# Deformable sampling with its first product in PSUM and one turning matmul per sample, and expert choice with piecewise exponentials and four early weight groups

## The chip, the cores and the metric

The kernel runs on one core of a Trainium2 chip. A core has a matrix engine (TensorE, PE in the profile), VectorE (DVE), ScalarE (ACT), GpSimd (POOL) and SyncE (SP), which work side by side from queues of their own, each in order. SBUF is the working memory, PSUM the small memory into which TensorE writes, in eight banks of 2 KB per partition. The metric is device time in microseconds for one execution, the median of several runs.

## The reference

The program is a network of four layers on an image tensor x of shape (4, 128, 64, 64), in float32. Each layer adds a spatial part and a per-token part to x. The change touches the spatial part of layer 1 (a modulated deformable convolution) and the per-token part of layers 1 and 2 (expert choice). Cut to these:

```python
# layer 1, spatial: 9 taps k, per pixel an offset (dy, dx) and a mask
y0 = jnp.floor(py).astype(jnp.int32); x0 = jnp.floor(px).astype(jnp.int32)
ly = py - y0; lx = px - x0
v00 = sample(y0, x0);     v01 = sample(y0, x0 + 1)
v10 = sample(y0 + 1, x0); v11 = sample(y0 + 1, x0 + 1)
sampled = v00*(1-wy)*(1-wx) + v01*(1-wy)*wx + v10*wy*(1-wx) + v11*wy*wx
sampled = sampled * mask[:, None]
out = jnp.einsum('bckhw,ock->bohw', sampled, weight.reshape(O, C, KK)) + bias

# layers 1 and 2, per token: 64 experts choose 8 tokens each out of 4096
logits = jnp.einsum('bsd,ed->bse', x, gate_w) + gate_b
probs = jax.nn.softmax(logits, axis=1)
vals, idx = jax.lax.top_k(probs.transpose(0, 2, 1), K)
pooled = jnp.einsum('bked,bke->bed', gathered, topv)
h = jax.nn.gelu(jnp.einsum('ebd,edh->ebh', pooled_and_one, weight1), approximate=False)
out = jnp.einsum('ebh,eho->ebo', h_and_one, weight2)
# each expert's output, times topv, is added back at its 8 tokens
```

## The kernel before

The image stays in SBUF as `xs`, channels on the 128 partitions, in chunks of 512 pixels (8 chunks per image). The stages follow one another: involution, a recurrence, the deformable sampling, expert choice, a convolution, expert choice again, attention, and a last mixture of experts. The stages at hand keep the order of the source on TensorE, ScalarE, VectorE and GpSimd (`tc.manual_schedule(engines=ORDERED)`): what is written first is queued first on its engine, and semaphores order the engines among themselves.

**Deformable sampling** (`deformable`). For each image, `plan(b)` makes the normalised image, the offsets, the row indices `idx` and four weights `wq[0..3]` per pixel and tap, and writes a table to device memory in which one row of 512 floats holds the four neighbours of a pixel, 128 channels each. Then, for 8 chunks, 9 taps and 4 blocks of 128 pixels, `taken` gathers 128 rows by an indirect DMA into a tile `dcn_g` (one pixel per partition, L872; 1152 such gathers in all) and weights them. It works on a pair of blocks at a time:

- ScalarE multiplies neighbour 0 by its weight into an SBUF tile `dcn_one` (L886);
- VectorE multiplies neighbour 1 into a slot of the PSUM tile `dcn_part` (L889), adds neighbour 2 there (L892), and adds neighbour 3 with the result going to an SBUF tile `dcn_sum` (L897).

`joined` then lets TensorE turn both tiles, from pixels on partitions to channels on partitions, by products with the identity that add up in the PSUM tile `dcn_pt` (L912 and L913). Each float32 product appears in the profile as two matmul records. `turn_back` copies a full `dcn_pt` (four blocks) to `dcn_st` on ScalarE (L929), `convolve` multiplies by the tap's weights into `dcn_out` (L933), and `finish` adds the nine taps' sum to the image on VectorE (L939). The calls are delayed by a number of steps (`at(2, joined, ...)`, 6 for `turn_back`, 2 more for `convolve`, 4 more for `finish`), and after each step one small piece of `plan` for the next image is issued (`side`), so that squares, copies, transposes and the offset convolution of the next image lie between. `GATHERED` is the number of gather buffers. The PSUM banks are all taken: three for `dcn_pt`, two for `dcn_out`, two for `plan`, one for `dcn_part`.

**Expert choice** (`expert_choice`). Two images share one set of 128 partitions (64 experts each), called a pair p. Phase one makes layer-norm scales, the logits `chosen[p]` (128 x 4096), a table of tokens in device memory (`rows`), the eight largest per expert (`largest`), the softmax denominators (`exponentials`, L1164 for pair 0 in one instruction, L1170 for pair 1 in eight pieces), the gathered tokens (`ask`) and their weighted sums (`pool`). Phase two streams the experts' weights, 16 groups of four experts, two tiles of 1 MB per group (`load`, L1042 and L1044): `first`, `turn`, `second` and `hand` follow one another with a lag of one group each. `EARLY` groups are loaded in phase one into buffers of their own, and `LATE` more buffers exist in phase two only. Between the groups of phase two, `mark(p)` marks the eight largest logits and `choose(p)` turns them into exponentials, everything else into zero. For pair 0 the exponentials `exps` are those of phase one; for pair 1 they are made at g = 5 (L1334).

Of the kernel before, what the change touches and what calls it, by code (L numbers as in the profile page):

```python
# [17 lines left out]
F32 = mybir.dt.float32  # L18
# [3 lines left out]
AF = mybir.ActivationFunctionType  # L22
ALU = mybir.AluOpType
AX = mybir.AxisListType
# [4 lines left out]
P = 128  # L29
B, H, W = 4, 64, 64  # L30
N = H * W
CH = 512
NCH = N // CH
# [618 lines left out]
def deformable(net, sampling):  # L652
# [7 lines left out]
    tc, nc = net.tc, net.nc  # L660
# [2 lines left out]
    NO = 3 * KK  # L663
    Q4 = 4
    BANKS = {"pt": 3, "out": 2, "pd": 1, "pv": 1}
    GATHERED = 14
    tables, woff, boff = sampling.tables, sampling.woff, sampling.boff
    wk, bias, grids = sampling.wk, sampling.bias, sampling.grids
    with ExitStack() as ctx:
# [195 lines left out]
        def taken(m, two):  # L865


            rows, idx, wq, j, k = m
            gs = []
            for i in two:  # L870
                g = sb.tile([P, 4 * P], F32, name="dcn_g", tag="g", bufs=GATHERED)
                nc.gpsimd.indirect_dma_start(  # L872
                    out=g,
                    out_offset=None,
                    in_=rows,
                    in_offset=bass.IndirectOffsetOnAxis(ap=idx[:, j + i, k : k + 1], axis=0),
                )
                gs.append(g)

            def weight(q, i):  # L880
                return wq[q][:, j + i, k : k + 1]

            ones, sums = [], []
            for i, g in zip(two, gs):
                s = sb.tile([P, P], F32, name="dcn_one", tag="one", bufs=12)
                nc.scalar.activation(s, g[:, 0:P], AF.Copy, scale=weight(0, i))  # L886
                ones.append(s)
            for i, g in zip(two, gs):
                nc.vector.tensor_scalar_mul(parts[:, i % 2, :], g[:, P : 2 * P], weight(1, i))  # L889
            for i, g in zip(two, gs):  # L890
                part = parts[:, i % 2, :]
                nc.vector.scalar_tensor_tensor(  # L892
                    out=part, in0=g[:, 2 * P : 3 * P], scalar=weight(2, i), in1=part, op0=ALU.mult, op1=ALU.add
                )
            for i, g in zip(two, gs):
                s = sb.tile([P, P], F32, name="dcn_sum", tag="sum", bufs=11)
                nc.vector.scalar_tensor_tensor(  # L897
                    out=s,
                    in0=g[:, 3 * P : 4 * P],
                    scalar=weight(3, i),  # L900
                    in1=parts[:, i % 2, :],
                    op0=ALU.mult,
                    op1=ALU.add,
                )
                sums.append(s)
            return ones, sums

        def joined(pt, two, ones, sums):

            for i, one_, s in zip(two, ones, sums):  # L910
                out = pt[:, i * P : (i + 1) * P]
                nc.tensor.matmul(out, one_, net.ident, start=i == 0, stop=False)  # L912
                nc.tensor.matmul(out, s, net.ident, start=False, stop=i == 3)  # L913

        parts = ps.tile([P, 2, P], F32, name="dcn_part", bufs=1)
        with tc.manual_schedule(engines=ORDERED):
            for _ in plan(0):
                pass
            side = iter(())

            later = {}
            n = 0

            def at(lag, do, *args):
                later.setdefault(n + lag, []).append(partial(do, *args))

            def turn_back(k, pt, po, b, c):
                st = sb.tile([P, CH], F32, name="dcn_st", tag="st")
                nc.scalar.copy(st, pt)  # L929
                at(2, convolve, k, st, po, b, c)  # L930

            def convolve(k, st, po, b, c):
                nc.tensor.matmul(po, wk[:, k, :], st, start=k == 0, stop=k == KK - 1)  # L933
                if k == KK - 1:
                    at(4, finish, b, c, po)

            def finish(b, c, po):
                xo = net.chunk(b, c)
                nc.vector.scalar_tensor_tensor(out=xo, in0=po, scalar=bias, in1=xo, op0=ALU.add, op1=ALU.add)  # L939

            def step():
                nonlocal n
                n += 1
                for do in later.pop(n, ()):
                    do()
                next(side, None)

            for b in range(B):
                for _ in side:
                    pass  # L950
                side = plan(b + 1) if b + 1 < B else iter(())
                rows, idx, wq = made.pop(b)
                for c in range(NCH):
                    po = ps.tile([P, CH], F32, name="dcn_out", tag="out", bufs=BANKS["out"])
                    for k in range(KK):
                        pt = ps.tile([P, CH], F32, name="dcn_pt", tag="pt", bufs=BANKS["pt"])
                        for i in range(0, 4, 2):
                            two = (i, i + 1)
                            at(2, joined, pt, two, *taken((rows, idx, wq, 4 * c, k), two))
                            if i:  # L960
                                at(6, turn_back, k, pt, po, b, c)
                            step()
            while later:
                step()


def expert_choice(net, layer):
# [13 lines left out]
    tc, nc, ins = net.tc, net.nc, net.ins  # L981
# [4 lines left out]
    CG = P // EG  # L986
    PAIRS = B // 2
    K, ROW = 8, P + 16
    EARLY, LATE = 3, 2
    GONE = -3.0e38  # L990
    w1, w2 = ins[f"L{layer}_ffn_weight1"], ins[f"L{layer}_ffn_weight2"]
    with ExitStack() as ctx:
# [22 lines left out]
        chosen = [keep.tile([P, N], F32, name=f"moe_chosen{i}") for i in range(PAIRS)]  # L1015
        totals = [keep.tile([P, 1], F32, name=f"moe_total{i}") for i in range(PAIRS)]
        cgate = keep.tile([D, E], F32, name="moe_cgate")
        exps = keep.tile([P, N], F32, name="moe_exp")

        behind = keep.tile([P, 1], F32, name="moe_behind")  # L1020
        nc.gpsimd.memset(behind[0:E], 0.0)
# [5 lines left out]
        def mark(p):  # L1027
            lg = chosen[p]
            nc.vector.match_replace(out=lg, in_to_replace=tops[p], in_values=lg, imm_value=GONE)

        def choose(p):

            lg = chosen[p]
            nc.vector.scalar_tensor_tensor(
                out=lg, in0=lg, scalar=GONE, in1=exps, op0=ALU.is_equal, op1=ALU.mult
            )
# [11 lines left out]
        with (  # L1048
# [109 lines left out]
                nc.vector.tensor_copy(places[p], row)  # L1158
                nc.vector.tensor_scalar_mul(negs[p], top[:, 0:1], -1.0)

            def exponentials(p):

                if p == 0:
                    nc.scalar.activation(exps, chosen[p], AF.Exp, bias=negs[p], accum_out=totals[p])  # L1164
                else:
                    sums = sb.tile([P, NCH], F32, name="moe_sums", bufs=1)
                    for c in range(NCH):
                        sq = sb.tile([P, CH], F32, name="moe_sq", tag="moe_sq", bufs=5)
                        lg = chosen[p][:, c * CH : (c + 1) * CH]
                        nc.scalar.activation(sq, lg, AF.Exp, bias=negs[p], accum_out=sums[:, c : c + 1])  # L1170
                    nc.vector.tensor_reduce(totals[p], sums, AX.X, ALU.add)
                shares[p] = sb.tile([P, K], F32, name="moe_share", tag="moe_share")
                nc.scalar.activation(shares[p], tops[p], AF.Exp, bias=negs[p])

            def ask(p, j):
                if j == 0:
# [47 lines left out]
                if j % 3 == 0:  # L1224
                    rows(0, j // 3 - 2)
            scales(1)
            exponentials(0)
            inverted(1)
            for c in range(4, NCH):
                rows(0, c)  # L1230
            turn_scales(1)
            for c in range(NCH):
                logits(1, c)
                for n in (2 * c, 2 * c + 1):
                    rows(1 + n // NCH, n % NCH)
            largest(1)
            for c in range(NCH):
                rows(3, c)
                ask(0, c)
            exponentials(1)  # L1240
            for j in range(K):
                ask(1, j)
            pool(0)
# [9 lines left out]
        with (  # L1253
# [55 lines left out]
            def hand(g, out):  # L1309
                for p in range(PAIRS):  # L1310
# [5 lines left out]
                        stop=g == GROUPS - 1 and p == PAIRS - 1,  # L1316
                    )

            hs, t2, act, outs = {}, {}, {}, {}
            for g in range(GROUPS + 3):  # L1320
                if g < GROUPS:
                    hs[g], t2[g] = first(g)
                if 0 <= g - 1 < GROUPS:
                    act[g - 1] = turn(g - 1, hs.pop(g - 1))
                if 0 <= g - 2 < GROUPS:
                    outs[g - 2] = second(g - 2, act.pop(g - 2), t2.pop(g - 2))
                if 0 <= g - 3:
                    hand(g - 3, outs.pop(g - 3))
                if g == 2:
                    mark(0)  # L1330
                if g == 4:
                    choose(0)
                if g == 5:
                    nc.scalar.activation(exps, chosen[1], AF.Exp, bias=negs[1])  # L1334
                if g == 7:
                    mark(1)
                if g == 9:
                    choose(1)
            for p in range(PAIRS):
                nc.vector.tensor_add(ots[p], handed[:, p, :], b2)  # L1340
                nc.vector.tensor_scalar_mul(ots[p], ots[p], totals[p])
# [701 lines left out]
```

## Time and profile before

| what | value |
|---|---|
| median of 3 runs | 8143.69 us (8137.75 to 8143.82) |
| the profiled execution, its own time | 8494.04 us |
| its span, first to last instruction | 8492.0 us |
| granted TensorE clock, mean over the span | 0.936 |
| busy: PE, DVE, ACT, POOL | 90%, 65%, 44%, 62% |
| gathers of the sampling stage (L872), first to last start | 1311.3 to 3096.8 us |
| in 1311 to 3097 us: PE, DVE, ACT, POOL busy | 1204, 1246, 548, 1089 us |
| the same stretch: granted clock, DMA share, GB/s | 0.79, 0.63, 184 |
| expert choice of layer 1, phase one (3116 to 3239 us) | PE 104, DVE 45, ACT 72 us busy, DMA share 0.46 |
| expert choice of layer 1, phase two (3239 to 3318 us) | PE 61, DVE 27, ACT 21 us busy, DMA share 0.95 |

A line of the groups reads: line in the kernel, engine, operation, output and inputs, shape, count; then busy time in us and the mean of one in ns; then the idle time of the engine just before these instructions and what ended it. A line of the timeline reads: start in us, length in us, engine, line, operation, count of merged instructions, and in brackets the engine's idle time before it with what released it. The engine that is busiest over the whole span need not bound a stage: in the sampling stage no engine is busy more than 70% of the time, and the spacing of successive instructions has to be looked at. The profiled execution is one execution, and it is slower than the timed ones by 350.35 us.

### The profile page before, as it was taken

Reading aid. Unit: us, or ns where it says so; the run is one execution under the profiler, and the core shown is the slowest. Engines: PE = TensorE matmul, PEld = TensorE weight load, DVE = VectorE, ACT = ScalarE, POOL = GpSimd, SP = SyncE. Lnnn points to the kernel's source line nnn. Section 1 sums busy time; section 2 is a strip of 40 time slices with the busy share of each in tenths; the row PEclk is TensorE's granted clock in tenths of the full one; section 3 lists DMA queues with packets and bytes.
Section 4 is the critical chain, followed back from the end, with each engine's and each line's share of the span. In section 5 each row is a group of like instructions: output and inputs, shape, how many; then the busy total and the mean of one; then the engine's idle time right before and its main releaser. Section 6 shows DMA issues by size and latency. Waiting matters only on the chain.

```text
span 8492.0 us, 144746 instructions
## 1 busy us (share of the span) xinstructions
PE 7639.5 (90%) x58958; PEld 3304.7 (39%) x58958; DVE 5545.6 (65%) x8706; ACT 3707.0 (44%) x7214; POOL 5264.3 (62%) x3014
## 2 busy tenths in 40 slices
PE   8999985767676678988999999999999999999989
PEld 2222243444444444433344344443444434444333
DVE  7888755777777654235667667776776766777255
ACT  4444432333332332041555555555555555555511
POOL 5889704656566630000788788887888868888800
PEclk9999997888787788997999999999999999999999
DMA  5443206656566545032454454554454544555400
GB/s 176 93 86 78 62 8 177 199 165 209 166 202 185 173 146 202 0 114 77 87 111 103 102 108 101 108 109 99 106 110 106 104 103 101 107 110 109 101 24 24
DMA packets 298170, 966.23 MB, mean 114 GB/s; under 512 B 42508, under 2 KB 112652, under 8 KB 239644
## 3 DMA queue, kind: packets, MB, share of 16 engines
q0 software_dynamic: 143872, 673.55, 33.7%
q1 hardware_dynamic: 153628, 283.40, 11.8%
q8 instruction: 463, 7.59, 0.4%
q14 instruction: 207, 1.70, 0.1%
HBM read 469.14 MB, written 85.01 MB: 65 GB/s over the span
## 4 chain that ended last, share of the span: by engine, by line
PE 51%; DVE 2%; issue 1%; DMA 1%; ACT 0%; POOL 0%; SPq 0%; POOLq 0%; ACTq 0%; DVEq 0%; another core or an unknown queue 0%
PE att_pv L1647 15%; PE att_sc L1734 13%; PE att_mx L1591 10%; PE att_sc L1635 5%; PE top_po L1947 3%; PE top_pw L1923 1%; DVE att_most L1602 1%; DMA moe_w<-in_L_ffn_weight 1%; PE att_sc L1564 1%; PE att_sc L1695 0%; PE top_po L1945 0%; PE att_sc L1678 0%; PE att_mx L1489 0%; PE att_sc L1525 0%; PE att_sc L1591 0%
## 5 line engine op out<-in xcount | busy, mean ns | idle before, releaser
L1666 POOL TENSOR_TENSOR att_acc<-att_acc,att_ex 128x2048 f32<-128x2048 f32 x640 | 2904.3, 4538 | 638.9 <-ACT att_ex L1735 619.6
L1602 DVE TENSOR_REDUCE att_most<-att_mx 128x2 f32<-128x1024 f32 x2016 | 2462.4, 1222 | 1073.5 <-PE att_mx L1591 990.6
L1735 ACT ACTIVATE att_ex<-att_sc 128x512 f32<-128x512 f32 x4096 | 2222.9, 595 | 1777.0 <-PE att_sc L1734 1493.8
L1734 PE MATMUL att_sc<-att_q,att_k 32*128 32x512 f32 x8192 | 2456.7, 606 | 0.0
L1591 PE MATMUL att_mx<-att_k,att_q 32*128 32x512 f32 x8064 | 2293.4, 647 | 13.0 <-DVE att_parts L1614 10.9
L872 POOL DMA_INDIRECT dcn_g<-dcn_table,dcn_idx x1152 | 1090.1, 946 | 763.1 <-issue 235.4
L1635 PE MATMUL att_sc<-att_rows,att_ones_b 32*128 32x256 bf16 (+1 forms) x6144 | 1502.9, 306 | 4.7 <-ACT att_ex L1735 4.7
L1647 PE MATMUL att_pv<-att_ex,att_vals 128*32 128x256 f32 x16384 | 1310.3, 391 | 0.0
L1591 PEld LDWEIGHTS att_mx<-att_k,att_q 32*128 32x128 f32 x8064 | 611.6, 185 | 869.3 <-issue 709.9
L410 POOL TENSOR_TENSOR inv_prod<-inv_seen,inv_prod 128x512 f32<-128x512 f32 (+1 forms) x672 | 837.6, 1274 | 95.8 <-ACT inv_prod L409 95.8
L412 DVE SCALAR_TENSOR_TENSOR inv_prod<-inv_pk,bspan,inv_seen 128x512 f32<-128x512 f32 (+1 forms) x1120 | 774.6, 743 | 142.0 <-PE inv_pk L399 141.7
L1647 PEld LDWEIGHTS att_pv<-att_ex,att_vals 128*32 128x32 f32 x16384 | 322.6, 108 | 1319.7 <-issue 1301.6
L1734 PEld LDWEIGHTS att_sc<-att_q,att_k 32*128 32x128 f32 x8192 | 818.7, 183 | 11.0 <-issue 8.3
L912 PE MATMUL dcn_pt<-ident,dcn_one 128*128 128x128 f32 x2304 | 531.0, 314 | 241.1 <-issue 108.6
L913 PE MATMUL dcn_pt<-ident,dcn_sum 128*128 128x128 f32 x2304 | 529.9, 312 | 157.5 <-issue 108.4
L409 ACT ACTIVATE inv_prod<-inv_pk,bspan 128x512 f32<-128x512 f32 (+1 forms) x672 | 436.1, 682 | 505.7 <-PE inv_pk L399 495.8
L912 PEld LDWEIGHTS dcn_pt<-ident,dcn_one 128*128 128x128 f32 x2304 | 440.0, 223 | 511.1 <-issue 313.5
L929 ACT COPY dcn_st<-dcn_pt 128x512 f32<-128x512 f32 x288 | 166.2, 577 | 880.4 <-remote 457.2
L399 PE MATMUL inv_pk<-inv_red,wtap 32*96 32x512 f32 (+1 forms) x3584 | 512.7, 638 | 7.4 <-DVE wtap L377 7.4
L897 DVE SCALAR_TENSOR_TENSOR dcn_sum<-dcn_g,dcn_w,dcn_part 128x128 f32<-128x128 f32 x1152 | 354.0, 345 | 253.1 <-remote 138.4
L421 PE MATMUL inv_out<-inv_prod,inv_fold 96*32 96x512 f32 (+1 forms) x3584 | 478.5, 605 | 8.5 <-DVE xs L429 8.5
L913 PEld LDWEIGHTS dcn_pt<-ident,dcn_sum 128*128 128x128 f32 x2304 | 413.8, 222 | 179.8 <-issue 116.5
(355 smaller groups left out, 7260.2 us busy)
## 6 DMA issues: line engine op xcount, KB each, us to landing
att_sum<-att_ex POOLq DMA_DIRECT2D x320, 1024.0 KB
inv_seen<-inv_image SPq DMA_DIRECT2D x256, 266.0 KB
moe_w<-in_L_ffn_weight SPq DMA_DIRECT2D x64, 1024.0 KB
dcn_table<-dcn_xt SPq DMA_DIRECT2D x32, 1024.0 KB
att_sum<-att_ex SPq DMA_DIRECT2D x32, 1024.0 KB
att_sum<-att_acc POOLq DMA_DIRECT2D x32, 1024.0 KB
dcn_g<-dcn_table,dcn_idx POOLq DMA_INDIRECT x1152
moe_table<-moe_xt SPq DMA_DIRECT2D x64, 288.0 KB
```

What stands on the lines that cost most here:

```text
L410: nc.gpsimd.tensor_mul(of, view, of)
L412: nc.vector.scalar_tensor_tensor(out=of, in0=as_shape(pk[0:m], of), scalar=by, in1=view, op0=ALU.add, op1=ALU.mult)
L872: nc.gpsimd.indirect_dma_start(out=g, out_offset=None, in_=rows, in_offset=bass.IndirectOffsetOnAxis(ap=idx[:, j + i, k : k + 1], axis=0),)
L912: nc.tensor.matmul(out, one_, net.ident, start=i == 0, stop=False)
L913: nc.tensor.matmul(out, s, net.ident, start=False, stop=i == 3)
L1591: nc.tensor.matmul(pm[i] if alone else pm[:, i, :], q[r, t * P : (t + 1) * P], ks[r, kc * CH : (kc + 1) * CH], start=True, stop=True,)
L1602: nc.vector.tensor_reduce(most[:, 2 * half : 2 * half + 2, kc], pm, AX.X, ALU.max)
L1635: nc.tensor.matmul(pe[:, cols], ones_b[r], lows[g][r, cols], start=cols.start == 0, stop=False)
L1647: nc.tensor.matmul(block["pv"][r, cols], vals[b][:, t, r], ex[:, h, cols], start=t == 0 and half == 0, stop=t == NT - 1 and half == 1,)
L1666: nc.gpsimd.tensor_add(block["acc"], block["acc"], ex)
L1734: nc.tensor.matmul(pe, ks[r, t * P : (t + 1) * P], qs[c][r], start=False, stop=True)
L1735: nc.scalar.activation(ex[:, h, :], pe, AF.Exp)
```

## The change

In the sampling, ScalarE's product of neighbour 0 goes into a slot of `dcn_part`, which has four slots instead of two. VectorE adds neighbours 1 and 2 there, and neighbour 3 with the result to `dcn_sum`. `dcn_one` is gone, and TensorE turns one tile per sample. The ring of `dcn_sum` grows from 11 to 15 tiles and that of the gathers from 14 to 16.

In the expert choice, pair 0's exponentials are made in eight pieces, four between the `rows` of pair 0 and four between the `logits` of pair 1; `denominators` adds the pieces' sums. `exps` (16 KB per partition) moves from the whole stage to phase two, where the exponentials of both pairs are made, at g = 1 and g = 6. Four groups of weights are loaded early instead of three, and one late buffer is left instead of two. `mark` and `choose` stay at g = 2 and 4 for pair 0, and at g = 7 and 9 for pair 1.

```diff
-    GATHERED = 14
+    SUMS = 15
+    GATHERED = 16
...
-            ones, sums = [], []
             for i, g in zip(two, gs):
-                s = sb.tile([P, P], F32, name="dcn_one", tag="one", bufs=12)
-                nc.scalar.activation(s, g[:, 0:P], AF.Copy, scale=weight(0, i))
-                ones.append(s)
-            for i, g in zip(two, gs):
-                nc.vector.tensor_scalar_mul(parts[:, i % 2, :], g[:, P : 2 * P], weight(1, i))
-            for i, g in zip(two, gs):
-                part = parts[:, i % 2, :]
-                nc.vector.scalar_tensor_tensor(
-                    out=part, in0=g[:, 2 * P : 3 * P], scalar=weight(2, i), in1=part, op0=ALU.mult, op1=ALU.add
-                )
+                nc.scalar.activation(parts[:, i, :], g[:, 0:P], AF.Copy, scale=weight(0, i))
+            for q in (1, 2):
+                for i, g in zip(two, gs):
+                    part = parts[:, i, :]
+                    nc.vector.scalar_tensor_tensor(
+                        out=part,
+                        in0=g[:, q * P : (q + 1) * P],
+                        scalar=weight(q, i),
+                        in1=part,
+                        op0=ALU.mult,
+                        op1=ALU.add,
+                    )
+            sums = []
             for i, g in zip(two, gs):
-                s = sb.tile([P, P], F32, name="dcn_sum", tag="sum", bufs=11)
+                s = sb.tile([P, P], F32, name="dcn_sum", tag="sum", bufs=SUMS)
                 nc.vector.scalar_tensor_tensor(
                     out=s,
                     in0=g[:, 3 * P : 4 * P],
                     scalar=weight(3, i),
-                    in1=parts[:, i % 2, :],
+                    in1=parts[:, i, :],
...
-            for i, one_, s in zip(two, ones, sums):
-                out = pt[:, i * P : (i + 1) * P]
-                nc.tensor.matmul(out, one_, net.ident, start=i == 0, stop=False)
-                nc.tensor.matmul(out, s, net.ident, start=False, stop=i == 3)
-
-        parts = ps.tile([P, 2, P], F32, name="dcn_part", bufs=1)
+            for i, s in zip(two, sums):
+                nc.tensor.matmul(pt[:, i * P : (i + 1) * P], s, net.ident, start=i == 0, stop=i == 3)
+
+        parts = ps.tile([P, 4, P], F32, name="dcn_part", bufs=1)
...
-    EARLY, LATE = 3, 2
+    EARLY, LATE = 4, 1
...
-        exps = keep.tile([P, N], F32, name="moe_exp")
...
+            sums = [sb.tile([P, NCH], F32, name=f"moe_sums{p}", bufs=1) for p in range(PAIRS)]
+
+            def exponentials(p, c):
+
+                sq = sb.tile([P, CH], F32, name="moe_sq", tag="moe_sq", bufs=5)
+                lg = chosen[p][:, c * CH : (c + 1) * CH]
+                nc.scalar.activation(sq, lg, AF.Exp, bias=negs[p], accum_out=sums[p][:, c : c + 1])
+
+            def denominators(p):
                 shares[p] = sb.tile([P, K], F32, name="moe_share", tag="moe_share")
                 nc.scalar.activation(shares[p], tops[p], AF.Exp, bias=negs[p])
+                nc.vector.tensor_reduce(totals[p], sums[p], AX.X, ALU.add)
...
             scales(1)
-            exponentials(0)
             inverted(1)
             for c in range(4, NCH):
                 rows(0, c)
+                exponentials(0, c - 4)
             turn_scales(1)
             for c in range(NCH):
                 logits(1, c)
+                if c < 4:
+                    exponentials(0, c + 4)
                 for n in (2 * c, 2 * c + 1):
                     rows(1 + n // NCH, n % NCH)
+            denominators(0)
             largest(1)
             for c in range(NCH):
                 rows(3, c)
                 ask(0, c)
-            exponentials(1)
+            for c in range(NCH):
+                exponentials(1, c)
+            denominators(1)
...
+            exps = sb.tile([P, N], F32, name="moe_exp", bufs=1)
...
-                if g == 2:
-                    mark(0)
-                if g == 4:
-                    choose(0)
-                if g == 5:
-                    nc.scalar.activation(exps, chosen[1], AF.Exp, bias=negs[1])
-                if g == 7:
-                    mark(1)
-                if g == 9:
-                    choose(1)
+                for p in range(PAIRS):
+                    if g == 1 + 5 * p:
+                        nc.scalar.activation(exps, chosen[p], AF.Exp, bias=negs[p])
+                    if g == 2 + 5 * p:
+                        mark(p)
+                    if g == 4 + 5 * p:
+                        choose(p, exps)
```

More of the change, by code (lines that the diff above doesn't have):

```diff
@@ L905, in taken, with joined @@
                 sums.append(s)
-            return ones, sums
-        def joined(pt, two, ones, sums):
-            for i, one_, s in zip(two, ones, sums):
-                out = pt[:, i * P : (i + 1) * P]
-                nc.tensor.matmul(out, one_, net.ident, start=i == 0, stop=False)
-                nc.tensor.matmul(out, s, net.ident, start=False, stop=i == 3)
-        parts = ps.tile([P, 2, P], F32, name="dcn_part", bufs=1)
+            return sums
+        def joined(pt, two, sums):
+            for i, s in zip(two, sums):
+                nc.tensor.matmul(pt[:, i * P : (i + 1) * P], s, net.ident, start=i == 0, stop=i == 3)
+        parts = ps.tile([P, 4, P], F32, name="dcn_part", bufs=1)
         with tc.manual_schedule(engines=ORDERED):
@@ L958, in deformable @@
                             two = (i, i + 1)
-                            at(2, joined, pt, two, *taken((rows, idx, wq, 4 * c, k), two))
+                            at(2, joined, pt, two, taken((rows, idx, wq, 4 * c, k), two))
                             if i:
@@ L1029, in mark, with choose @@
             nc.vector.match_replace(out=lg, in_to_replace=tops[p], in_values=lg, imm_value=GONE)
-        def choose(p):
+        def choose(p, exps):
             lg = chosen[p]
@@ L1159, in largest @@
                 nc.vector.tensor_scalar_mul(negs[p], top[:, 0:1], -1.0)
[L1161 to L1171, printed above, removed]
+            sums = [sb.tile([P, NCH], F32, name=f"moe_sums{p}", bufs=1) for p in range(PAIRS)]
[4 more added lines that the diff above has]
+            def denominators(p):
                 shares[p] = sb.tile([P, K], F32, name="moe_share", tag="moe_share")
                 nc.scalar.activation(shares[p], tops[p], AF.Exp, bias=negs[p])
+                nc.vector.tensor_reduce(totals[p], sums[p], AX.X, ALU.add)
             def ask(p, j):
```

## The prediction

> **What bounds the kernel now.** The timed runs have a median of 8143.69 us; the profiled execution took 8494.04 us, 350.35 us more. So I first ask which parts of the profile belong to the runs at all. The page gives the span and, among the costliest groups, the gathers of the sampling stage:
>
> ```profile
> span 8492.0 us, 144746 instructions
> ...
> L872 POOL DMA_INDIRECT dcn_g<-dcn_table,dcn_idx x1152 | 1090.1, 946 | 763.1 <-issue 235.4 <-DVE dcn_part L889 199.7 <-ACT dcn_one L886 98.6
> ```
>
> The groups of that stage alone (1295 to 3115 us) give its per-sample work:
>
> ```profile
> L892 DVE SCALAR_TENSOR_TENSOR dcn_part<-dcn_g,dcn_w,dcn_part 128x128 f32<-128x128 f32 x1152 | 409.9, 356 | 63.1 <-DVE dcn_part L889 12.4 <-DVE dcn_part L892 7.0 <-issue 4.1
> L889 DVE TENSOR_SCALAR dcn_part<-dcn_g,dcn_w 128x128 f32<-128x128 f32 x1152 | 404.9, 351 | 80.9 <-DMA dcn_g<-dcn_table,dcn_idx 18.4 <-DVE dcn_part L889 9.1 <-remote 8.9
> L886 ACT ACTIVATE dcn_one<-dcn_g,dcn_w 128x128 f32<-128x128 f32 x1152 | 376.3, 394 | 36.4 <-DMA dcn_g<-dcn_table,dcn_idx 34.0 <-issue 2.2
> ```
>
> Then the timeline of one undisturbed stretch, first VectorE, then GpSimd:
>
> ```profile
> 2952.69 0.74 DVE L889 TENSOR_SCALAR dcn_part<-dcn_g,dcn_w 128x128 f32<-128x128 f32 x2
> 2953.47 0.75 DVE L892 SCALAR_TENSOR_TENSOR dcn_part<-dcn_g,dcn_w,dcn_part 128x128 f32<-128x128 f32 x2
> 2954.32 0.61 DVE L897 SCALAR_TENSOR_TENSOR dcn_sum<-dcn_g,dcn_w,dcn_part 128x128 f32<-128x128 f32 x2
> 2954.97 0.74 DVE L889 TENSOR_SCALAR dcn_part<-dcn_g,dcn_w 128x128 f32<-128x128 f32 x2
> ```
>
> ```profile
> 2953.37 0.94 POOL L872 DMA_INDIRECT dcn_g<-dcn_table,dcn_idx  x1 [0.30 <-issue]
> 2954.61 0.95 POOL L872 DMA_INDIRECT dcn_g<-dcn_table,dcn_idx  x1 [0.30 <-issue]
> ```
>
> GpSimd starts a gather every 1.25 us (0.95 + 0.30). VectorE takes a pair of samples in 2.28 us (2952.69 to 2954.97), against 2.50 us for two gathers: GpSimd is the bound, VectorE close behind. 1152 x 1.25 = 1440 us, but the gathers run from 1311 to 3097 us, 1786 us. The rest is stretches like this one, where VectorE starts one instruction each 0.71 us whatever it is (TensorE does the same beside it):
>
> ```profile
> 2937.16 0.35 DVE L889 TENSOR_SCALAR dcn_part<-dcn_g,dcn_w 128x128 f32<-128x128 f32 x1 [1.43 <-DVE dcn_sum L897]
> 2937.88 0.35 DVE L889 TENSOR_SCALAR dcn_part<-dcn_g,dcn_w 128x128 f32<-128x128 f32 x1 [0.36 <-issue]
> 2938.59 0.35 DVE L892 SCALAR_TENSOR_TENSOR dcn_part<-dcn_g,dcn_w,dcn_part 128x128 f32<-128x128 f32 x1 [0.36 <-DVE dcn_part L889]
> ```
>
> Their sum: GpSimd's idle 763.1, less 66.8 for the first table (the wait on dcn_table in the view of dcn_g), less 1152 x 0.30 = 346, leaves 351 us. That is the 350 us by which the profiled execution exceeds the median. I read these stretches as a cost of recording, absent from timed runs, where the stage is 1440 us.
>
> **What the Trainium skill says.** "PSUM — Partial Sum Buffer", section on bank collisions: ScalarE and VectorE may not access the same bank and quadrant at once, even at different columns; order them by bank, not address. The trace agrees on the ordering: the two L889 of a pair write different halves of dcn_part yet are 0.39 us apart (0.74 - 0.35), like dependent operations, while the two L897, which write separate SBUF tiles, are 0.26 apart (0.61 - 0.35). So the program keeps order within dcn_part as a whole. "Perfetto Trace Analysis", Optimizing Scalar/DVE Operations: a ScalarE operation's fixed cost is about 93 ns on SBUF and 51 ns on PSUM; no instruction here shows a ScalarE write to PSUM.
>
> **The sampling change, step by step.** L886 now writes its product into dcn_part; VectorE adds three neighbours there, and TensorE turns one product per sample instead of two.
>
> 1. TensorE loses 2304 records of L912 (531 us busy). TensorE is not the bound: undisturbed it does a tap's 8 products and its L933 in about 2.65 us of the 5.00 that four gathers take. Gain in timed runs: 0. In the profile it also removes recorded instructions.
> 2. VectorE still has three operations per sample: L889 (351 ns) becomes one like L892 (356 ns). +5 ns.
> 3. The wait. dcn_part is 128 x 512 f32, 2 KB per partition, one bank, though it has four slots. Two engines now write it, so ScalarE's products for a pair wait for VectorE's last addition of the pair before, and VectorE's first addition waits for both products. Before, ScalarE ran up to 12 tiles ahead. Now ScalarE and VectorE alternate, once per pair.
>    - VectorE's part, start of its first addition to end of its last: from the 2.28 us period take 0.04 of gap: 2.24 us.
>    - ScalarE's part: two operations, no longer overlapped. 394 ns each into SBUF; less 42 ns for PSUM by the skill's figures, an estimate of 0.35 us. Bounds 0.31 (twice that saving) and 0.39 (none).
>    - Hand-overs are 0.03 us: VectorE to ScalarE
>
> ```profile
> 3143.47 0.69 DVE L1116 TENSOR_TENSOR moe_chosen<-moe_chosen,moe_pl 128x512 f32<-128x512 f32 x1 [1.84 <-PE moe_pl L1111]
> 3144.19 0.72 ACT L1117 ACTIVATE moe_chosen<-moe_chosen,moe_gbias 128x512 f32<-128x512 f32 x1 [1.23 <-DVE moe_chosen L1116]
> ```
>
>    and the same the other way (L1088 ends at 3136.96, L1092 starts at 3136.99). Three per pair (into ScalarE, between its two, out) 0.10, and 0.03 for a second wait on one instruction, as between L892 and L897.
>    - Sum: 2.24 + 0.70 + 0.13 = 3.07 us per pair, over GpSimd's 2.50. 576 x 3.07 = 1768 us.
>    - Queued behind the waiting L886 on ScalarE are L929 (0.58 us) and the next image's squares and copies (0.58 to 0.63). They run while VectorE adds (2.24 us) and cost nothing; if one waited itself, 0.58 x 288 = 167 us. VectorE's work on the next image runs while ScalarE multiplies (0.83 us); only the 0.95 us reciprocals and steps with a finish (0.75) beside another operation stick out: 24 x 0.12 + some 10 x 0.6 = 9 us, I take 10.
>    Stage: 1778 instead of 1440, +338 us.
> 4. SUMS 15 and GATHERED 16: with VectorE behind GpSimd, deeper rings only fill. 0.
>
> **The expert choice, twice.** Before, ScalarE's exponential over 4096 columns holds TensorE up:
>
> ```profile
> 3180.55 1.11 PE L1139 MATMUL moe_pt<-ident,xs 128*128 128x128 f32 x4 [5.09 <-ACT moe_xt L1141]
> ```
>
> In eight pieces (0.70 us each, row L1170; 5.6 against 3.7 us) between the copies, I estimate 3 of those 5 us back, less 4 x 0.3 us where four logits steps outgrow TensorE's 3.1 us period (ScalarE 2.7 + 0.7), less 0.3 for the shares: 1.5 us per layer. In the weights' loop the load queue runs without a break from 3239.0 to 3301.4 us (5.3 us per group of 2 MB, 13 groups). A fourth group loaded early takes 5.3 us off it; but with one late buffer the next group's second tile waits for second(0) (issued at 3247.8 before), some 1 us of empty queue, and the exponentials now made at g = 1 (3.7 us with two table loads of 1.28) delay second(1) and the load behind it by another 1 to 2. Net 3 us. The 1 MB pieces of the fourth group load beside phase one's light traffic. Together 2 x 4.5 = 9 us gained; bounds 20 gained and 5 lost.
>
> **Sum.** +338 - 9 = +329 on the median: 8143.69 + 329 = 8473 us. For the profiled execution: 8492 - 1786 + 1778 - 9 = 8475 us plus whatever recording still costs; with fewer records per us I expect 0 to 100. So its span should hardly move although the median rises 4%.
>
> **Rivals.**
> - ScalarE's side work ends up in the loop (L929 late every tap): +167, 8640 us. For: ScalarE's queue is in order. Against: 0.70 + 0.58 + 0.63 = 1.9 us of ScalarE work fits beside the 3.07.
> - Not slower, one mechanism: order in dcn_part is kept by slot. Then ScalarE works on two slots while VectorE adds in the others, GpSimd stays the bound, and the result is 8143.69 - 9 = 8135 us. It decides if a pair then takes under 2.50 us, which 2.28 does. For: four slots exist. Against: the 0.39 us spacing and the bank rule.
> - The 0.71 us stretches are real in timed runs and recording costs its 350 us elsewhere. Then the stage is 1786 before and 1778 after: 8144 - 8 - 9 = 8127 us, down to some 7950 if fewer TensorE instructions shorten stalls and the alternation fails too. Against: 351 equals 350, and I saw no such stretch in the expert choice.
>
> **Chances and range.** Alternation as forecast 0.79, with side work 0.08, order by slot 0.05, stalls real 0.08. A difference of 0.2% (16 us) is about what a measurement can tell from none. Faster 0.06, within 0.2% 0.06, slower 0.88. Range from the bounds of the pair: 2.24 + 0.62 + 0.10 = 2.96 and 2.24 + 0.78 + 0.16 = 3.18 us give 1705 to 1832 us, so +265 less 20, and +392 + 25 + 5: 8389 to 8566; I keep 8390 to 8565.
>
> **What would show it.** Right: gathers spaced 1.5 us on the mean, GpSimd waiting on VectorE; ScalarE's L886 shown waiting on VectorE's additions and VectorE's first addition on ScalarE, in turn, 3.0 to 3.15 us per pair; no TensorE wait of size; gathers over some 1780 us. Wrong: pairs at 2.3 us with L886 running ahead, or the median unmoved.

## The result and the profile after

The changed kernel takes 8443.58 us (median of 4 runs, 8440.63 to 8449.95) against 8140.83 us for the kernel before (4 runs, 8137.75 to 8143.82): ratio 1.0371, 95% interval 1.0358 to 1.0384, or +302.8 us. The profiled execution of the changed kernel took 8441.53 us, 2 us from its median. That of the kernel before, shown above, had been 350 us over its own; whether these 350 us appear differed from chip to chip, and is taken up in the experiments. This section compares with the 8141 us.

The page's span, then the groups of the sampling stage (1295 to 3090 us):

```profile
span 8439.4 us, 141304 instructions
...
L873 POOL DMA_INDIRECT dcn_g<-dcn_table,dcn_idx x1152 | 1092.4, 948 | 723.1 <-ACT dcn_part L885 464.9 <-DVE dcn_part L889 161.8 <-DMA dcn_table<-dcn_xt 68.2
L889 DVE SCALAR_TENSOR_TENSOR dcn_part<-dcn_g,dcn_w,dcn_part 128x128 f32<-128x128 f32 x2304 | 820.2, 356 | 464.0 <-ACT dcn_part L885 399.6
L914 PE MATMUL dcn_pt<-ident,dcn_sum 128*128 128x128 f32 x2304 | 574.5, 391 | 625.0 <-DVE dcn_sum L900 614.6
L885 ACT ACTIVATE dcn_part<-dcn_g,dcn_w 128x128 f32<-128x128 f32 x1152 | 427.8, 371 | 1151.8 <-DVE dcn_sum L900 1109.3 <-DMA dcn_g<-dcn_table,dcn_idx 23.9
```

The last column is the reading. Before, GpSimd's releasers were mixed and ScalarE waited for gathers. Now ScalarE's product (L885) waits 1109 of its 1152 idle us for VectorE's last addition (L900); VectorE's additions (L889) wait 400 us for ScalarE's product; GpSimd waits for both, because the gathered tiles come free later; TensorE (L914) waits 615 us for the finished sums. The durations of single operations on VectorE and GpSimd have hardly moved.

The timeline shows the turn-taking, VectorE first, then ScalarE, then GpSimd (start, duration, engine and line, count, and in brackets the idle time before it):

```profile
2800.43 1.53 DVE L889 SCALAR_TENSOR_TENSOR dcn_part<-dcn_g,dcn_w,dcn_part 128x128 f32<-128x128 f32 x4 [0.84 <-ACT dcn_part L885]
2802.07 0.61 DVE L900 SCALAR_TENSOR_TENSOR dcn_sum<-dcn_g,dcn_w,dcn_part 128x128 f32<-128x128 f32 x2
2803.51 1.53 DVE L889 SCALAR_TENSOR_TENSOR dcn_part<-dcn_g,dcn_w,dcn_part 128x128 f32<-128x128 f32 x4 [0.84 <-ACT dcn_part L885]
```

```profile
2800.33 0.58 ACT L930 COPY dcn_st<-dcn_pt 128x512 f32<-128x512 f32 x1
2802.70 0.78 ACT L885 ACTIVATE dcn_part<-dcn_g,dcn_w 128x128 f32<-128x128 f32 x2 [1.79 <-DVE dcn_sum L900]
2805.79 0.77 ACT L885 ACTIVATE dcn_part<-dcn_g,dcn_w 128x128 f32<-128x128 f32 x2 [2.31 <-DVE dcn_sum L900]
```

```profile
2803.15 0.94 POOL L873 DMA_INDIRECT dcn_g<-dcn_table,dcn_idx  x1 [0.89 <-ACT dcn_part L885]
2804.40 0.95 POOL L873 DMA_INDIRECT dcn_g<-dcn_table,dcn_idx  x1 [0.30 <-DVE dcn_part L889]
2806.24 0.95 POOL L873 DMA_INDIRECT dcn_g<-dcn_table,dcn_idx  x1 [0.89 <-ACT dcn_part L885]
```

A pair takes 2803.51 - 2800.43 = 3.08 us. VectorE works 2.24 or 2.25 us of it (to 2802.68), ScalarE starts 0.02 us later and holds the tile for 0.78 us, and VectorE starts again 0.03 us after it. The copy L930 runs while VectorE adds, as forecast. GpSimd starts two gathers per 3.08 us, where it could start one each 1.25 us. From first gather to last it takes 3054.1 - 1307.7 = 1746.4 us.

### The profile page after: what moved, and what is told of

Its sections match the earlier page's. It is cut to its first block, busy times and chain, and to the rows that moved or that the text cites. A ratio compares the mean times of both kernels' runs of the same rounds, so it can differ in the third digit from the quotient of the medians.

```text
span 8439.4 us, 141304 instructions
## 1 busy us (share of the span) xinstructions
PE 7565.7 (90%) x56654; PEld 3047.2 (36%) x56654; DVE 5554.7 (66%) x8708; ACT 3799.7 (45%) x7248; POOL 5265.5 (62%) x3014
## 4 chain that ended last, share of the span: by engine, by line
PE 57%; DVE 3%; issue 1%; DMA 1%; ACT 1%; POOL 0%; SPq 0%; ACTq 0%; POOLq 0%; DVEq 0%
PE att_pv L1649 15%; PE att_sc L1736 13%; PE att_mx L1593 10%; PE att_sc L1637 5%; PE conv_po L1403 3%; PE top_po L1949 3%; DMA moe_w<-in_L_ffn_weight 1%; PE top_pw L1925 1%; DVE att_most L1604 1%; PE moe_pd L1065 1%; PE att_sc L1566 0%; DVE xs L1355 0%; PE att_sc L1697 0%; PE att_sc L1680 0%; PE top_po L1947 0%
## 5 line engine op out<-in xcount | busy, mean ns | idle before, releaser
L914 PE MATMUL dcn_pt<-ident,dcn_sum 128*128 128x128 f32 x2304 | 574.5, 391 | 625.0 <-DVE dcn_sum L900 614.6
L889 DVE SCALAR_TENSOR_TENSOR dcn_part<-dcn_g,dcn_w,dcn_part 128x128 f32<-128x128 f32 x2304 | 820.2, 356 | 464.0 <-ACT dcn_part L885 399.6
L885 ACT ACTIVATE dcn_part<-dcn_g,dcn_w 128x128 f32<-128x128 f32 x1152 | 427.8, 371 | 1151.8 <-DVE dcn_sum L900 1109.3
L914 PEld LDWEIGHTS dcn_pt<-ident,dcn_sum 128*128 128x128 f32 x2304 | 439.5, 266 | 1147.9 <-issue 622.7
L934 PE MATMUL dcn_out<-dcn_st,dcn_wk 128*128 128x512 f32 x576 | 473.2, 919 | 0.0
L1637 PEld LDWEIGHTS <-att_ones_b 32*128 32x128 bf16 x6144 | 382.2, 91 | 95.1 <-issue 33.3
```

The lines of the kernel that those rows point to most:

```text
L889: nc.vector.scalar_tensor_tensor(out=part, in0=g[:, q * P : (q + 1) * P], scalar=weight(q, i), in1=part, op0=ALU.mult, op1=ALU.add,)
L914: nc.tensor.matmul(pt[:, i * P : (i + 1) * P], s, net.ident, start=i == 0, stop=i == 3)
L1637: nc.tensor.matmul(pe[:, cols], ones_b[r], lows[g][r, cols], start=cols.start == 0, stop=False)
```

## The experiments

The last four kernels ran on chips on which the kernel before takes 8508 or 8509 us; the first eight on chips on which it takes 8142 or 8143 us. Ratios are always against the kernel before on the same chip. Each of these four chips was used at one time only, so the runs do not separate the chip from the hour; "on such a chip" is meant with this reservation. On which chip the first profile of the kernel before was taken is not on record.

**The product in SBUF.** ScalarE's product goes to a ring of twelve SBUF tiles, as before the change, and VectorE's first addition reads it from there. TensorE still turns one product per sample.

```diff
-                nc.scalar.activation(parts[:, i, :], g[:, 0:P], AF.Copy, scale=weight(0, i))
+                one_ = sb.tile([P, P], F32, name="dcn_one", tag="one", bufs=12)
+                nc.scalar.activation(one_, g[:, 0:P], AF.Copy, scale=weight(0, i))
...
-                        in1=part,
+                        in1=one_ if q == 1 else part,
```

> The changed kernel, but ScalarE's product goes into an SBUF tile again (ring of 12) and VectorE's first addition reads it from there; still one turning product per sample; rings of sums and gathers back at 11 and 14. Theory (ScalarE and VectorE alternate because both write one PSUM bank): the alternation is gone, a pair takes VectorE about 2.3 us, GpSimd's 1.25 us per gather is the bound again, 8141 less the some 11 us of the expert choice = 8130 us (8115 to 8150). Rival (the loss comes from VectorE's new first addition or the single turning product, not from the bank): it stays at 8440. On the profile: if the 0.71 us stretches of the kernel before are a cost of recording, the profiled execution may again be longer than the timed ones, by less than 350 us, since TensorE leaves half the records.

Measured: 8136.93 us (8131.65 to 8142.89) against 8142.13; ratio 0.9994, interval 0.9986 to 1.0003. ScalarE's product waits mostly for gathers again (378 of its 487 idle us), VectorE's first addition only 30 us for ScalarE, and GpSimd is back at one gather each 1.25 us:

```profile
2601.48 0.95 POOL L873 DMA_INDIRECT dcn_g<-dcn_table,dcn_idx  x1 [0.30 <-DMA dcn_g<-dcn_table,dcn_idx]
2602.73 0.95 POOL L873 DMA_INDIRECT dcn_g<-dcn_table,dcn_idx  x1 [0.30 <-DMA dcn_g<-dcn_table,dcn_idx]
```

The gathers take 1458.7 us, 7 more than in the undisturbed profile of the kernel before (1451.7, below). The whole loss goes away with the place where ScalarE writes. And with half of TensorE's turning gone and nothing else in the way, there is no gain from it either.

**The expert choice alone.** The sampling of the kernel before, the expert choice of the changed one.

> The sampling of the kernel before with the expert choice of the changed kernel. Theory: 8141 - 11 = 8130 us (8124 to 8137), the gain that the two stages show in the traces (2.5 and 8.6 us). Rival (the expert choice pays back what it gains, or part of the 303 us lies there): 8141 or more. The profiled execution should be some 350 us longer than the timed ones, as before, since the sampling is unchanged.

Measured: 8129.44 us (8117.49 to 8134.83); ratio 0.9983, interval 0.9976 to 0.999, 13 us less. Its profiled execution took 8117.49 us: the 350 us more that were expected of it are not there.

**Two accumulator tiles.** The four slots are split into two tiles of one bank each; for the bank, dcn_pt's ring goes from 3 to 2 and its copy comes two steps earlier.

```diff
-    BANKS = {"pt": 3, "out": 2, "pd": 1, "pv": 1}
+    BANKS = {"pt": 2, "out": 2, "pd": 1, "pv": 1}
...
-        parts = ps.tile([P, 4, P], F32, name="dcn_part", bufs=1)
+        parts = [ps.tile([P, 2, P], F32, name=f"dcn_part{h}", bufs=1) for h in range(2)]
...
-                                at(6, turn_back, k, pt, po, b, c)
+                                at(4, turn_back, k, pt, po, b, c)
```

> The changed kernel with the four slots in two PSUM banks, one for each pair of blocks; the bank comes from the ring of turned blocks (two instead of three), whose copies back come two steps sooner. Theory (order is kept by bank): ScalarE writes one bank while VectorE adds in the other, so its two products (0.78 us) and the hand-overs lie beside VectorE's 2.24 us and GpSimd is the bound: 8130 us, up to 8180 if the shorter ring of turned blocks makes TensorE wait. Rival (the wait is for the engine, not for the bank, or ScalarE's side work fills the loop): 8400 or more.

Measured: 8128.49 us (8122.73 to 8142.3); ratio 0.9985, interval 0.9977 to 0.9993. The group of ScalarE's product and VectorE's timeline:

```profile
L885 ACT ACTIVATE dcn_part<-dcn_g,dcn_w 128x128 f32<-128x128 f32 x1152 | 427.2, 371 | 816.0 <-DMA dcn_g<-dcn_table,dcn_idx 467.6 <-DVE dcn_sum L900 288.6 <-DVE dcn_part L889 50.8
```

```profile
2599.93 1.53 DVE L889 SCALAR_TENSOR_TENSOR dcn_part<-dcn_g,dcn_w,dcn_part 128x128 f32<-128x128 f32 x4 [0.19 <-ACT dcn_part L885]
2601.57 0.60 DVE L900 SCALAR_TENSOR_TENSOR dcn_sum<-dcn_g,dcn_w,dcn_part 128x128 f32<-128x128 f32 x2
2602.27 1.53 DVE L889 SCALAR_TENSOR_TENSOR dcn_part<-dcn_g,dcn_w,dcn_part 128x128 f32<-128x128 f32 x4
```

ScalarE waits for gathers more than for VectorE, and this pair takes 2602.27 - 2599.93 = 2.34 us. On the mean a pair takes 2.52 us, as GpSimd's gathers set it (1449.0 us from first to last, 576 pairs). ScalarE now fills one tile while VectorE adds in the other. This version and the expert choice alone are 0.15 to 0.17% under the kernel before, and some 314 us under the changed kernel. It keeps the deeper rings of the change, so these are not what costs.

**The product written twice.** Each product of ScalarE is made two times over, to put a price on ScalarE's share of the turn.

```diff
-                nc.scalar.activation(parts[:, i, :], g[:, 0:P], AF.Copy, scale=weight(0, i))
+                for _ in range(2):
+                    nc.scalar.activation(parts[:, i, :], g[:, 0:P], AF.Copy, scale=weight(0, i))
```

> The changed kernel with ScalarE's product of each sample made twice into the same slot. Theory (ScalarE's time stands in series with VectorE's): two more operations of 0.41 us start to start per pair, 576 x 0.81 = 467 us more, about 8910 us, and pairs of 3.9 us. Rival (ScalarE's time is partly hidden): less than 8700.

Measured: 8908.04 us (two runs, 8904.25 and 8911.83), 464 over the changed kernel; ratio 1.0939, interval 1.0919 to 1.0959.

```profile
2601.25 1.58 ACT L886 ACTIVATE dcn_part<-dcn_g,dcn_w 128x128 f32<-128x128 f32 x4 [1.79 <-DVE dcn_sum L901]
2602.77 0.58 ACT L931 COPY dcn_st<-dcn_pt 128x512 f32<-128x512 f32 x1
2605.13 1.58 ACT L886 ACTIVATE dcn_part<-dcn_g,dcn_w 128x128 f32<-128x128 f32 x4 [1.79 <-DVE dcn_sum L901]
```

The four products take 1.58 us where two took 0.78, and the period grows by the same 0.80, from 3.08 to 3.88 us: 576 x 0.80 = 461 us. ScalarE's time adds to the period in full; if it had run beside VectorE, these products would have cost little.

**Two slots instead of four.**

```diff
-                nc.scalar.activation(parts[:, i, :], g[:, 0:P], AF.Copy, scale=weight(0, i))
+                nc.scalar.activation(parts[:, i % 2, :], g[:, 0:P], AF.Copy, scale=weight(0, i))
...
-        parts = ps.tile([P, 4, P], F32, name="dcn_part", bufs=1)
+        parts = ps.tile([P, 2, P], F32, name="dcn_part", bufs=1)
```

> The changed kernel with two slots in the tile of partial sums, as before, instead of four (both pairs of blocks use the same two). Theory (order is kept by the bank, so the number of slots in it is of no matter): 8444 us as the changed kernel, within 0.2%, pairs of 3.08 us. Rival (order is kept by slot, and four slots give ScalarE some room): slower than the changed kernel by part of ScalarE's 0.8 us per pair, 8500 or more.

Measured: 8445.52 us (8438.18 to 8450.89); ratio 1.037, interval 1.0354 to 1.0386, as with four. The second pair of slots buys nothing.

**The kernel before, profiled once more.**

> The kernel before, profiled once more. My reading in the prediction: the 0.71 us stretches are a cost of recording; then this profiled execution is again some 350 us longer than the timed ones and its gathers take some 1786 us from first to last. Rival (they belonged to that one execution, as the profiled executions of the four kernels run since suggest, none of which has them): 8142 us within 15, gathers in some 1448 us.

Measured: 8140.74 us in its profiled execution, on the median of its timed runs. The page's span and the groups of the gathers and of ScalarE's product:

```profile
span 8138.8 us, 144746 instructions
...
L872 POOL DMA_INDIRECT dcn_g<-dcn_table,dcn_idx x1152 | 1092.3, 948 | 427.2 <-DMA dcn_g<-dcn_table,dcn_idx 98.6 <-issue 79.8 <-DMA dcn_table<-dcn_xt 66.8
L886 ACT ACTIVATE dcn_one<-dcn_g,dcn_w 128x128 f32<-128x128 f32 x1152 | 451.1, 400 | 695.3 <-DMA dcn_g<-dcn_table,dcn_idx 689.3 <-DVE dcn_part L892 1.0 <-DVE dcn_part L889 0.8
```

GpSimd's idle time is 427 us, of which 346 are gaps of 0.30 and 67 the first table: 14 us are left where the profile used for the prediction had 351. Recording alone doesn't make the stretches of 0.71 us. ScalarE waits for gathers alone. With this profile both kernels can be compared stage by stage. The window of the gathers in each (of this kernel all but the last six), the changed kernel first (us; busy us and count of PE, PEld, DVE, ACT, POOL; granted TensorE clock; DMA share; GB/s):

```profile
1308.00:3054.00 1746.00, 1144.15 (x3624) 584.27 (x3624) 1253.23 (x3614) 623.03 (x1522) 1091.20 (x1151) 0.69 0.65 188
```

```profile
1305.00:2752.00 1447.00, 1113.23 (x5916) 759.69 (x5916) 1242.09 (x3629) 629.66 (x1528) 1086.60 (x1146) 0.94 0.76 226
```

VectorE, ScalarE and GpSimd do nearly the same amount of work in both, spread over 299 us more.

**Three groups of weights early.** The expert choice alone, with EARLY, LATE = 3, 2 as before.

> The sampling of the kernel before, the expert choice of the changed kernel, but three groups of weights early and two late buffers as before. Theory (of the expert choice's gain of 12 us about half comes from the fourth early group, some 3 us per layer, the rest from the exponentials in pieces): 8129 + 6 = 8135 us (8131 to 8139). Rivals: the fourth group is worth nothing, 8129; or all of it, 8141.

Measured: 8135.2 us (8125.71 to 8145.2) against 8143.27; ratio 0.999, interval 0.9982 to 0.9999. Against the 0.9983 with four groups early, about half of the gain is from the pieces and half from the fourth group; the intervals overlap, so the split is rough. The stage times of the profiles agree: phase two, from its first matmul to the first sum added to the image, takes 80.3 and 80.2 us with three in the two layers, 77.6 and 77.0 with four.

**One addition less on VectorE.** The expert choice alone, without VectorE's addition of the third neighbour (L892 of the kernel before); that part of the sum is left out.

> The sampling of the kernel before with the expert choice of the changed kernel, leaving out VectorE's addition of the third neighbour (two operations of 0.39 us less per pair of samples, so the samples lack that part). Theory (GpSimd's 1.25 us per gather is the bound of the sampling before the change): no faster by more than 15 us than the same kernel with the addition, 8114 to 8132 us. Rival (VectorE's 2.28 us per pair is the bound, or shares it): faster by up to 576 x 0.78 = 449 us.

Measured: 8127.17 us (8119.14 to 8138.93); ratio 0.9981, interval 0.9974 to 0.9988, the same as with the addition (0.9983). So VectorE, 2.28 of 2.50 us busy, does not bound the kernel before. That GpSimd's issue does is read from its gathers, which follow each other at 1.25 us; no run made them shorter.

**One tile of two banks.** The version with two accumulator tiles, but the two banks belong to one tile.

```diff
-                nc.scalar.activation(parts[i // 2][:, i % 2, :], g[:, 0:P], AF.Copy, scale=weight(0, i))
+                nc.scalar.activation(parts[:, i // 2, i % 2, :], g[:, 0:P], AF.Copy, scale=weight(0, i))
...
-        parts = [ps.tile([P, 2, P], F32, name=f"dcn_part{h}", bufs=1) for h in range(2)]
+        parts = ps.tile([P, 2, 4, P], F32, name="dcn_part", bufs=1)
```

> The two-bank kernel again, but the four slots belong to one accumulator tile of two banks (slots 0 and 1 in the first, 2 and 3 in the second) instead of two tiles. If the order between ScalarE and VectorE is kept bank by bank, this is the same as two tiles: about 8130 us (8120 to 8140), gathers over some 1450 us. If the order is kept for the whole tile, the alternation is back: pairs every 3.08 us, 8444 us.

Measured: 8472.66 us (8469.34 to 8476.71) against 8509.35; ratio 0.9956, interval 0.994 to 0.9973. Neither number was among those expected, because on this chip the kernel before takes 366 us longer. The trace decides all the same:

```profile
2808.91 1.53 DVE L889 SCALAR_TENSOR_TENSOR dcn_part<-dcn_g,dcn_w,dcn_part 128x128 f32<-128x128 f32 x4 [0.84 <-ACT dcn_part L885]
2810.55 0.60 DVE L900 SCALAR_TENSOR_TENSOR dcn_sum<-dcn_g,dcn_w,dcn_part 128x128 f32<-128x128 f32 x2
2812.00 1.53 DVE L889 SCALAR_TENSOR_TENSOR dcn_part<-dcn_g,dcn_w,dcn_part 128x128 f32<-128x128 f32 x4 [0.84 <-ACT dcn_part L885]
```

The pairs are 3.09 us apart, with the same 0.84 us for ScalarE's turn, although ScalarE writes another bank than VectorE. So the order is kept for the tile as a whole, not for the bank. Both versions have the shorter ring of dcn_pt and the earlier copy; they differ in the tile alone. The traces hold no addresses: which bank a slot lies in is taken from the shapes in the program. Whether two tiles inside one bank would run freely wasn't tried.

**The changed kernel, the kernel before, and the two tiles on such a chip.** All three ran on one chip, on which the kernel before takes 8507.69 us (8497.86 to 8522.55, 16 runs).

> The changed kernel, unchanged, timed again beside the kernel before, because on the chip of the last run the kernel before took 8509 us, not 8143. If the chip shows the stretches of 0.71 us per instruction (before at 8500 or more), they are a property of the chip and not of recording: then the changed kernel, whose period of 3.08 us hides most of them, takes about 8470 us, some 0.4% less than before. If the chip shows none, 8444 against 8143 as at first.

> The kernel before, profiled on the same chip. Where its timed runs are near 8509 us, its profiled execution is too, with about 350 us of GpSimd idle time in the sampling stage beyond 346 us of gaps and 67 us for the first table; where they are near 8143 us, about 15 us.

> The kernel with the slots in two accumulator tiles, on the same chip. If the stretches come from the number of instructions that TensorE has to be given (2304 fewer matmuls here), it loses clearly less than the kernel before on a chip that shows them: 8250 to 8400 us against 8509. If they strike every instruction alike on VectorE and GpSimd, it takes about 8490 us. On a chip without them, 8128 us.

Measured: the changed kernel 8476.81 us (8471.12 to 8484.06), ratio 0.9958, interval 0.9942 to 0.9975. There it is 31 us faster than the kernel before. The kernel before took 8521.54 us in its profiled execution; two tiles took 8504.97 us (8485.68 to 8522.56), ratio 0.9997, interval 0.9988 to 1.0007. The group of the gathers of the kernel before on this chip, then its timeline in one stretch: VectorE, ScalarE and GpSimd:

```profile
L872 POOL DMA_INDIRECT dcn_g<-dcn_table,dcn_idx x1152 | 1093.6, 949 | 783.6 <-issue 222.7 <-DVE dcn_part L889 190.8 <-ACT dcn_one L886 115.1
```

```profile
2977.35 0.36 DVE L892 SCALAR_TENSOR_TENSOR dcn_part<-dcn_g,dcn_w,dcn_part 128x128 f32<-128x128 f32 x1 [0.36 <-DVE dcn_part L889]
2978.08 0.35 DVE L892 SCALAR_TENSOR_TENSOR dcn_part<-dcn_g,dcn_w,dcn_part 128x128 f32<-128x128 f32 x1 [0.37 <-DVE dcn_part L892]
2979.54 0.35 DVE L897 SCALAR_TENSOR_TENSOR dcn_sum<-dcn_g,dcn_w,dcn_part 128x128 f32<-128x128 f32 x1 [1.10 <-DVE dcn_part L892]
```

```profile
2966.56 1.28 ACT L886 ACTIVATE dcn_one<-dcn_g,dcn_w 128x128 f32<-128x128 f32 x4
2980.22 0.59 ACT L929 COPY dcn_st<-dcn_pt 128x512 f32<-128x512 f32 x1 [12.38 <-remote]
```

```profile
2976.83 0.95 POOL L872 DMA_INDIRECT dcn_g<-dcn_table,dcn_idx  x1 [0.30 <-issue]
2981.38 0.95 POOL L872 DMA_INDIRECT dcn_g<-dcn_table,dcn_idx  x1 [3.60 <-DVE dcn_part L889]
```

The stretches are back, 783.6 - 66.8 - 346 = 371 us of GpSimd idle time beyond the gaps, and the timed runs are as long as the profiled one. VectorE's operations start 0.73 and 1.46 us apart, ScalarE starts nothing for 12.4 us, and GpSimd in the end waits 3.6 us for the tiles. In the changed kernel the gathers take 3087.2 - 1310.7 = 1776.5 us here, only 30 more than on the first chip. The trace shows why. Taken from the start of one pair's second sum (L900, or L897 of the kernel before) to that of the next, seven of its 575 periods are over 4 us, together 30 us more than 3.08 each; nine in ten stay under 3.1 us. The kernel before has 90 periods over 4 us on this chip, two tiles have 97. So the stretches do not fall into the waits of the alternating kernel unseen; most of them do not occur in it. With two tiles they cost the full amount (8504.97 - 8128.49 = 376 us), although TensorE has 2304 matmuls fewer; so the number of TensorE's instructions does not set them. What holds the engines up in these stretches, and why the alternating kernel has so few, the profile does not show, and it stays open.

## Why the prediction was right, and where it was not

The forecast was 8473 us, +329; the runs gave 8443.58 us, +303, within the range, and by the mechanism named. That these runs fell on a chip without the stretches was luck: on one with them the same change gave -31.

- Step 3, the alternation: right, and nearly to the digit. A pair was worked out at 3.07 us and takes 3.08. ScalarE's product is 0.371 us, not 0.35: the saving of 42 ns, an estimate from the Trainium skill's "Perfetto Trace Analysis", Optimizing Scalar/DVE Operations, was 29 ns here, from 400 to 371. VectorE's part is 2.24 to 2.25 as taken; the hand-overs are two of 0.02 to 0.03, and the extra 0.03 of a second wait isn't there. These misses cancel, so the agreement to 0.01 us is partly luck. The product in SBUF, two tiles and the product written twice show the alternation from three sides. The reason given was half right: "the program keeps order within dcn_part as a whole" held, but the spacing of 0.39 us that was to show it is between VectorE's own instructions and says nothing of two engines. Nor did the remark that dcn_part is one bank carry it, or the section on bank collisions in the Trainium skill's "PSUM — Partial Sum Buffer": one tile of two banks alternates just the same. No run was made to let both engines into one bank at once, so that section's rule, to order by bank, is neither shown nor refuted here.
- The term mis-sized is the stage before, "1440" us. On the first chips it is 1451.7 us from first gather to last and 9.9 us more to the expert choice, 1462. The changed kernel's stage was put at 1778 us and takes 1746.4 + 28.1 = 1774.5. So the difference is +313 and not +338: the 14 us of idle time that even an undisturbed stage has, and its tail, were left out on one side of the subtraction.
- Steps 1, 2 and 4: no surprise. TensorE's saving is worth nothing (product in SBUF, 0.9994) and VectorE's 5 ns are in the period; the deeper rings were not tried alone. "If one waited itself" did not happen: L930 lies beside VectorE's additions. The 10 us of VectorE's own side work can't be seen: the mean pair, 3.06 us (L900 starts from 1314.6 to 3076.6 us), is no longer than the one shown.
- The signs: the pair's period, the turn-taking and the spacing of the gathers (1.52 us on the mean) came as named. Two did not come as worded: "GpSimd waiting on VectorE" is 162 us, against 465 for ScalarE (gaps of 0.30 us included), and where "no TensorE wait of size" was expected, TensorE waits 615 us for the sums. That costs nothing, since VectorE waits only 1.4 us for TensorE in the whole stage.
- The expert choice: 9 us forecast; the two layers went from 226.1 to 221.6 and from 222.8 to 217.5 us between the second profile of the kernel before and the changed one, 9.8 together. With the +313 that is +303, the measured difference; so close a match is luck, for the same code took 216.4 and 216.0 us in the profile of the expert choice alone, 16.5 less than before. The fourth group is worth some 3 us per layer in phase two, as said (the loads, though, run on after the last one is issued at 3301.4 us: 13 groups of 5.3 us are 69 us, and the first is issued at 3239.0), and the late second tile is there too, in the times at which SyncE issues the weights, with ScalarE's exponential below them:

```profile
3208.02 0.37 SPq L1042 DMA_DIRECT2D moe_w<-in_L_ffn_weight  x1
3212.20 0.37 SPq L1044 DMA_DIRECT2D moe_w<-in_L_ffn_weight  x1
3212.61 0.64 SPq L1042 DMA_DIRECT2D moe_w<-in_L_ffn_weight  x1
3220.10 0.37 SPq L1044 DMA_DIRECT2D moe_w<-in_L_ffn_weight  x1
```

```profile
3212.35 3.71 ACT L1336 ACTIVATE moe_exp<-moe_chosen,moe_neg 128x4096 f32<-128x4096 f32 x1
```

- "A cost of recording, absent from timed runs": wrong. The stretches were absent from the timed runs at hand, so 1440 us was near enough for them; but recording is not their cause, for six profiled executions of kernels without the alternation on the first chips are no longer than their timed runs, and the timed runs on the last chips are as long as those with the stretches in their profile. On those the third rival describes what happens: it put the change at 17 us faster, from a stage of 1786 against 1778 us and the 9 of the expert choice; measured 31 us faster, from gathers over 3116.9 - 1307.4 = 1809.5 against 1776.5 us. That the profiled execution should hardly move (8475 us and up to 100 more) while the median rises 4% fell with it: it took 8441.53 us, and on one chip profiled and timed executions move together.

So "3.7% slower" belongs to chips without the stretches. The alternating period of 3.08 us is seen on both kinds; what it costs depends on what the kernel before takes there.

## What to carry to other kernels

Before an operation's output is moved into a tile that another engine works on, look how far the producer runs ahead: a single tile written by both made them take turns here, with two slots or four and over one bank or two, and the price is the sum of both engines' times plus hand-overs against the present bound. A second tile, or a ring in SBUF, kept them apart. When a profiled execution lies far from the timed runs, profile again, and on another chip, before the excess is explained: the same change was 3.7% slower on one chip and 0.4% faster on another.

## What the runs showed of the hardware beyond that

In the window of the gathers the granted TensorE clock was 0.94 before and 0.69 after the change, with 3624 matmuls in 1746 us instead of 5916 in 1447. The mean turning matmul took 391 ns after (L914) and 309 before (L913). Two fifths fewer matmuls kept TensorE busy for about as long (1144 against 1113 us). It costs nothing here, since TensorE doesn't bound the stage. With nearly the same matmuls the granted clock was 0.81 over 1446 us (two tiles, 3644 of them), 0.69 over these 1746 us, and 0.61 over 2200 us (the product written twice, 3624). So it fell as the same work was spread out, not with the number of matmuls alone; whether the idle time is the cause was not tried by itself.
